# An attention layer over sorted edges: parts of 96, 51 and 40 groups in two stacked tables instead of three parts of 165, 142 and 96

## The chip, the cores and the metric

One Trainium2 chip; the kernel runs on one of its eight cores. The metric is the device time of one execution in microseconds (us). A core has a matmul engine (PE, with a weight load of its own, PEld), a vector engine (DVE), a scalar engine (ACT), GpSimd (POOL) and a queue that only issues transfers (SP); sixteen DMA engines move the bytes between HBM and the on-chip memory.

## The reference

A graph layer with 12,500 nodes of 128 features and 412,500 edges, sorted by target node:

```python
q = x @ Wq + bq;  k = x @ Wk + bk;  v = x @ Wv + bv;  h = x @ Wn + bn
eh = edge_attr @ We + be                                   # 64 -> 128 features
hmid = leaky_relu(concat([q[src], k[dst], eh]) @ A1 + b1, 0.2)
scores = leaky_relu(hmid @ A2 + b2, 0.2)                   # 8 heads
w = softmax(scores.mean(-1), axis=0)                       # over all edges
out = segment_sum(w[:, None] * v[dst], src, num_segments=n)
y = layernorm(h + out) * gamma + beta
return layernorm(x + y)
```

The softmax runs over all edges, and the sum goes back to the *source* node, while the edges come sorted by *target*. So the kernel has to sort 412,500 records by source.

## The kernel before

**Two streams of work.** *Making* goes through the edges in 403 groups of 1024 (`make`, one pass of six steps a group). For a group it loads the edge features (`eat`), a window of 128 rows of the k and v table (`kvs`) and target indices (`dstb`), multiplies them with one-hot matrices on PE (`pkv`), copies the product with ACT into a record buffer (`rec`, six of them, four tiles of 128 records each; L946 and L947), and POOL scatters each tile with an indirect DMA into a table in HBM (`rtab`, L958): eight scatters a group. A record is 260 floats. The table has 98 stretches, one for each block of source nodes, and each stretch has room for a number of tiles of 128 records. Where in its block's stretch a record goes is counted as the edges pass (`count`, `masked`, `places` on PE and DVE).

*Summing* (`sums_of`) reads the tables back. A *unit* is three blocks with the same `t` tiles each (15 tiles for `t` of 5, 12 for `t` of 4; the last unit of a round has two blocks). For a unit SP loads the records (`rt`), the q rows (`qs`), the old partial sum (`old`) and a row of source indices (`rowB`). PE, ACT and DVE then work in pieces of four tiles: the hidden layer (`ph`, `hm`), the scores (`psc`), a running maximum (`mx`, `m`, `ref`), the exponentials (`w`), and the weighted sum by source (`ohs`, `ohw`, `psm`), which is added to `old` and stored to `atab`. In the code, `lags` and `last_lags` give for each kind of instruction the step at which it stands, by the number of four-tile pieces `nk`.

**Parts and rounds.** Records can't all wait until the end, so making is cut into *parts* (`PARTS`, in groups), and a part's stretch of a table is read back in *rounds*. A part's last number is its end; the numbers ahead of it are *stops*, at which the first tiles of every block are surely full and a round may already read them. Part 0 and 2 use table 0, part 1 table 1 (`p % TABS`). What lies beyond a block's own records in a part's last round is masked (`masks`, made in `ended` at the part's end); in the first two parts, which find the tables unwritten, the last tiles of each stretch are filled with zeros beforehand (`fill`, from `empty` on chip or `zeros` in HBM). A part's end also closes one matmul accumulation of counts (`pc`) and opens the next, with the check of limits between (`ended`, `begin`).

**What sets the order.** Everything is in program order on each engine; no scheduler moves it. The summing steps are spread over the making steps: a round begins at its stop or end, or when the round before it is through at 12 tiles a group, whichever is later:

```python
free_at = max(free_at, g)
begun.append(free_at)
free_at += sum(len(bs) * t + 2.4 for q, bs, _ in units if q == p) / PACE
```

With 33 units a round that is 39.3 groups for `t` = 4 and 47.4 for `t` = 5. Rounds begin at groups 74, 140, 187.4, 234.8, 278, 317.3, 367 and 406.3, so 8% of round 6 and the whole of round 7 are left when making ends; these steps run alone, as the *tail*. In the tail a copy of `x + beta` for the end is also made (`rows_x`, `moved`, `put_x`: 14 pieces, 12 steps apart), and then `closing` normalizes and writes the output. During the first groups, before the first round, making runs beside the *preparation*: the q, k, v and h tables (`tables`) and the edge lists (`later`), spread over nine tenths of the groups up to the first stop, and the fills.

The text speaks of these lines of the kernel before: L818, L827, L838 (SP loads of making), L572 (fills), L800 and L880 (counts on PE), L931 and L936 (making on PE), L946 and L947 (record copies on ACT), L958 (scatters), L1144, L1159, L1198, L1356, L1404 (SP's transfers of a unit), L1188 (`slT`), L1224 and L1233 (hidden layer), L1258 (scores), L1284 (heads), L1299 (maximum of a unit), L1305, L1314 and L1323 (reference and weights), L1375 (weighted sum), L1468 (copies of `x`), L1699 (subtractions in the preparation).

Of the kernel before, what the change touches and what calls it, by code (L numbers as in the profile page):

```python
# [21 lines left out]
P = 128  # L22
# [6 lines left out]
GT = 8  # L29
# [3 lines left out]
ROWS = 3  # L33
XA = 3
SPAN = 42
PARTS = (74, 140, 165), (225, 278, 307), (367, 403)
NP = len(PARTS)
NR = sum(map(len, PARTS))
PACE = 12
TABS = 2  # L40
# [9 lines left out]
class Plan:  # L50
# [4 lines left out]
    def __init__(self, n, e, nb, groups):  # L55
        self.n, self.e, self.nb, self.groups = n, e, nb, groups
        at = lambda c: groups * c // 403
        ends = [at(part[-1]) for part in PARTS]
        self.parts = list(zip([0] + ends[:-1], ends))

        def means(g0, g1):
            return [
                (min(e, g1 * GT * P) - g0 * GT * P) * max(0, -(-(n - b) // nb)) / n
                for b in range(nb)
            ]

# [14 lines left out]
        self.lo = [[(most - f) * P for f in fill] for fill in self.fill]  # L81
        self.gate = max(
            g for g in range(self.parts[0][1])
            if all(m + 4.5 * m**0.5 <= lo for m, lo in zip(means(0, g), self.lo[0]))
        )

        self.rounds = []
        for p, (g0, g1) in enumerate(self.parts):
            t0 = 0
            for g in map(at, PARTS[p][:-1]):  # L90
                t = int(min(m - 4.4 * m**0.5 for m in means(g0, g)) // P) - t0
                assert t > 0
                self.rounds.append((p, g, t0, t))
                t0 += t
            self.rounds.append((p, g1, t0, self.tiles[p] - t0))

    def bounds(self):

        first = np.arange(self.nb + 1) * self.cap
        out = [first] * NP  # L100
        for p, g, t0, t in self.rounds:
            full = np.array([(t0 + t) * P] * self.nb + [0])
# [369 lines left out]
def sorted_path(  # L472
# [22 lines left out]
    rtab = [dram.tile([plan.rows, WR], FP, name=f"rtab{k}") for k in range(TABS)]  # L495
# [292 lines left out]
    pcs = {}  # L788
    ready, made_rows = {}, [1]
    masks, placed, lims = {}, {}, {}  # L790
    last_rounds = [r for r, q in enumerate(plan.rounds) if q[1] == plan.parts[q[0]][1]]
    for t in sorted({plan.rounds[r][3] for r in last_rounds}):
        placed[t] = const.tile([P, t], FP, name=f"placed{t}")
# [11 lines left out]
    def make(p):  # L805
# [136 lines left out]
        def evacuate(g, j, pk):  # L942
# [11 lines left out]
            for h in range(2):  # L954
                for i in range(2):
                    t = h * (GT // 2) + j + i
                    nc.gpsimd.nop()
                    one_tile = nc.gpsimd.indirect_dma_start(  # L958
                        out=rtab[p % TABS][:, :],
                        out_offset=bass.IndirectOffsetOnAxis(ap=idxs[g][:, t : t + 1], axis=0),  # L960
                        in_=rec[:, i, h, :], in_offset=None,
                    ).ins
# [143 lines left out]
    def sums_of(bp):  # L1106
# [32 lines left out]
        def load(i):  # L1139
            r, bs, t = units[i]  # L1140
            cap, n, m = plan.cap, plans[i][0], len(bs)
            p, _, t0, _ = plan.rounds[r]
            rt = (late["blk"] if spare_buffer(i) else bp).tile([P, TM, WR], FP, name="rt")
            rows_in = nc.sync.dma_start(  # L1144
                out=rt[:, :n, :].rearrange("p (u t) w -> p u (t w)", u=m),
                in_=rtab[p % TABS][bs[0] * cap : (bs[0] + m) * cap, :]
                .rearrange("(u c) w -> u c w", u=m)[:, t0 * P : (t0 + t) * P, :]
                .rearrange("u (p t) w -> p u (t w)", p=P),
            ).ins
            of_part = [k for k, q in enumerate(plan.rounds) if q[0] == p]  # L1150
            for k in range(of_part.index(r) + 1, len(of_part)):
                tc.declare_no_dep(rows_in, group=f"rows{p}.{k}", reason="tiles that are full")
            tc.add_to_no_dep_group(f"loads{p}.{of_part.index(r)}", rows_in)
            state[i] = dict(rt=rt, hm={}, oh={}, sel={})

        def load_q(i):
# [755 lines left out]
```

## Time and profile before

| | |
|---|---|
| median of 3 runs | 4827.88 us (4826.07 to 4830.85) |
| the profiled execution | 4829.19 us, span 4827.2 us |
| busy share of the span | PE 83%, PEld 64%, DVE 84%, ACT 65%, POOL 68% |
| first and last scatter | 59.3 and 4282.7 us |
| first and last unit's maximum (L1299) | 932.2 and 4685.8 us |
| mean granted clock of PE | 0.916 of full speed |
| DMA | 1484.41 MB, mean 308 GB/s |

The profiled execution is one of its own, with a trace; its span runs from the first to the last instruction. PE's busy share is a sum of modelled matmul ends, so it is an upper figure. Rows of groups read: line, engine, operation, tiles written and read, form, count | busy us, mean ns | idle before, and who ended it. Rows of waits read: who waited for whom: us in total, times, longest. A share over the span mixes three stages: making alone, making beside summing, and the tail.

### The profile page before, as it was taken

What the parts mean: (1) busy time and instruction counts of PE and PEld (TensorE: products, weight loads), DVE (VectorE), ACT (ScalarE), POOL (GpSimd) and SP (SyncE); (2) the same over time, 40 slices, a digit from 0 to 9 for tenths busy, and PEclk for the clock granted to TensorE, in tenths of its full rate; (3) what the DMA queues carried; (4) which work ended last, traced back from release to release, by engine and by line L of the source; (5) the groups of instructions that cost most, each with busy time, mean ns of one, the idle gap of its engine ahead of it and who ended that gap; (6) DMA issues with size and microseconds to landing.
All of it is one profiled execution on the core that took longest, in us unless ns stands there. A gap on an engine that the chain in (4) does not pass through costs nothing. (4 is left out here: it accounts for less than half of the span.)

```text
span 4827.2 us, 84360 instructions
## 1 busy us (share of the span) xinstructions
PE 3991.6 (83%) x26680; PEld 3111.2 (64%) x26680; DVE 4064.7 (84%) x8217; ACT 3144.8 (65%) x8198; POOL 3304.4 (68%) x3279
## 2 busy tenths in 40 slices
PE   3556655577788999999999999998998899998997
PEld 2334433466666777777777666666777777666777
DVE  8878886688878999999998888888999988877767
ACT  2432222366666778787787777777777777777886
POOL 3777777777777777777777777777777777741103
PEclk7877785899888999999999999999999999999999
DMA  6888887888988999999999999999999999989964
GB/s 196 282 279 288 286 298 243 294 300 298 296 299 299 358 336 334 333 348 337 323 335 324 329 331 329 332 336 325 342 332 326 333 316 334 320 294 327 318 215 176
DMA packets 599153, 1484.41 MB, mean 308 GB/s; under 512 B 100352, under 2 KB 299923, under 8 KB 596902
## 3 DMA queue, kind: packets, MB, share of 16 engines
q1 hardware_dynamic: 436350, 1049.04, 65.4%
q0 software_dynamic: 154752, 429.39, 23.3%
q8 instruction: 212, 3.47, 0.3%
q14 instruction: 247, 2.02, 0.1%
q10 hardware_dynamic: 7592, 0.48, 0.1%
HBM read 906.61 MB, written 611.06 MB: 314 GB/s over the span
## 5 line engine op out<-in xcount | busy, mean ns | idle before, releaser
L958 POOL DMA_INDIRECT rtab<-rec,idx x3224 | 3219.2, 999 | 1061.2 <-issue 777.2
L946 ACT ACTIVATE rec<-pkv 128x1024 f32<-128x1024 f32 x806 | 822.2, 1020 | 1120.4 <-DMA rtab<-rec,idx 572.8
L1346 ACT ACTIVATE ohw<-ohs,w 128x128 f32<-128x128 bf16 x3626 | 1189.1, 399 | 75.7 <-DVE ohs L1332 27.2
L1375 PE MATMUL psm<-rt,ohw 128*128 128x128 f32 x7252 | 1023.1, 285 | 1.1 <-ACT ohw L1346 1.0
L1375 PEld LDWEIGHTS psm<-rt,ohw 128*128 128x128 f32 x7252 | 943.9, 197 | 76.1 <-ACT hm L1243 7.7
L936 PE MATMUL pkv<-WeS,eat 128*128 128x256 f32 x3224 | 946.4, 421 | 0.0
L1247 DVE TENSOR_TENSOR hm<-ph,hm 128x512 f32<-128x512 f32 (+1 forms) x949 | 627.4, 661 | 300.9 <-ACT hm L1243 299.0
L931 PE MATMUL pkv<-kvs,ohd 128*128 128x256 bf16 x3224 | 539.1, 295 | 373.6 <-ACT rec L946 370.2
L931 PEld LDWEIGHTS <-ohd 128*128 128x128 bf16 x3224 | 320.9, 105 | 645.9 <-issue 531.8
L936 PEld LDWEIGHTS pkv<-WeS,eat 128*128 128x128 f32 x3224 | 620.2, 214 | 75.0
L1224 PE MATMUL ph<-ident,rt 128*128 128x128 f32 x3626 | 587.2, 284 | 64.5 <-DVE hm L1247 63.6
L1210 DVE TENSOR_SCALAR ohT<-rowB,iotaP,power 128x512 bf16<-128x512 uint8 (+2 forms) x1274 | 598.9, 492 | 34.8 <-DMA rowB<-row 34.6
L1243 ACT ACTIVATE hm<-ph 128x512 f32<-128x512 f32 (+1 forms) x949 | 537.5, 566 | 84.1 <-PE ph L1233 29.2
L1224 PEld LDWEIGHTS ph<-ident,rt 128*128 128x128 f32 x3626 | 418.3, 146 | 269.7 <-issue 145.5
L1233 PE MATMUL ph<-ohT,qs 128*128 128x512 bf16 (+2 forms) x2548 | 559.7, 323 | 16.1 <-DVE ohT L1210 11.3
L872 DVE TENSOR_SCALAR ohd<-dstb,node 128x1152 bf16<-128x1152 uint8 x404 | 565.0, 1399 | 4.5 <-PE pkv L931 4.5
L900 DVE TENSOR_TENSOR ats<-pc,oh 128x792 f32<-128x792 f32 x403 | 392.2, 973 | 61.7 <-PE pc L880 56.6
L1332 DVE TENSOR_TENSOR ohs<-iotaE,sl 128x512 bf16<-128x512 bf16 (+1 forms) x949 | 404.6, 426 | 5.0 <-ACT ohw L1346 4.8
L862 DVE TENSOR_REDUCE few<-oh 128x99 bf16<-128x792 bf16 x403 | 395.1, 980 | 13.9
L911 DVE TENSOR_REDUCE pos<-ats 128x8 f32<-128x792 f32 x403 | 390.7, 970 | 2.5
L1258 PE MATMUL psc<-hm,A2s 128*32 128x512 f32 (+1 forms) x1898 | 345.9, 607 | 31.9 <-DVE hm L1247 23.7
L1284 PEld LDWEIGHTS psm<-headsum,z 96*128 96x128 f32 (+2 forms) x2112 | 259.7, 193 | 32.8 <-issue 8.3
(190 smaller groups left out, 3790.5 us busy)
## 6 DMA issues: line engine op xcount, KB each, us to landing
rt<-rtab SPq DMA_DIRECT2D x160, 1950.0 KB
rt<-rtab SPq DMA_DIRECT2D x96, 1560.0 KB
eat<-in_ea SPq DMA_DIRECT2D x201, 512.0 KB
rtab<-rec,idx POOLq DMA_INDIRECT x3224
dstb<-dtab SPq DMA_DIRECT2D x201, 256.0 KB
qs<-qtab SPq DMA_DIRECT2D x256, 192.0 KB
atab<-old SPq DMA_DIRECT2D x256, 192.0 KB
old<-atab SPq DMA_DIRECT2D x224, 192.0 KB
```

Source lines behind the costliest of these rows:

```text
L872: nc.vector.tensor_scalar(to, row[:, cols], node, None, op0=ALU.is_equal)
L931: nc.tensor.matmul(pk[:, i, h, :], ohd[t], kvs, start=(h == 0), stop=False,)
L936: nc.tensor.matmul(pk[:, i, :, :D], eat[:, (j + i) * P : (j + i + 1) * P], WeS, start=False, stop=True,)
L946: nc.scalar.activation(rec[:, :, :, : 2 * D], pk, AF.Copy)
L958: one_tile = nc.gpsimd.indirect_dma_start(out=rtab[p % TABS][:, :], out_offset=bass.IndirectOffsetOnAxis(ap=idxs[g][:, t : t + 1], axis=0) ...
L1210: nc.vector.tensor_scalar(st["oh"][k][:, (a - t0) * P : (b - t0) * P], st["rowB"][:, a * P : b * P], iotaP, power[:, bs[u] : bs[u] + 1], o ...
L1224: nc.tensor.matmul(ph[:, j * P : (j + 1) * P], st["rt"][:, t0 + j, :D], ident, is_transpose=True, start=(j == 0), stop=False,)
L1233: nc.tensor.matmul(ph[:, cols], st["qs"][:, j0 // t, s, :], oh[:, cols], start=False, stop=(s == 1 and j1 == t0 + n),)
L1243: nc.scalar.activation(hm, state[i]["ph", k][:, : n * P], AF.Copy, scale=SLOPE)
L1247: nc.vector.tensor_tensor(hm, ph[:, : n * P], hm, op=ALU.max)
L1346: nc.scalar.activation(ohw[:, j, :], ohs[:, :, j], AF.Copy, scale=st["w"][:, t0 + j : t0 + j + 1])
L1375: nc.tensor.matmul(st["psS"][:, (1 + u) * P : (2 + u) * P], ohw[:, j, :], st["rt"][:, t0 + j, D : 2 * D], start=(k == 0), stop=(k == t - 1),)
```

## The change

Seven parts take the place of three. They end at groups 96, 192, 243, 283, 323, 363 and 403; the first two have a stop each, at 60 and 156. Rounds go from eight to nine, with 4, 5, 4, 5, 5, 4, 4, 4 and 4 tiles a block (before 5, 5, 5, 4, 4, 5, 4, 5): 39 tiles a block instead of 37, 297 units instead of 264. Stretches of a table are 9 tiles long instead of 15. Part 3 lies in table 0 above part 2's five tiles, part 5 in table 1 above part 4's four (`TABLE`, `ABOVE`); part 6 goes to the bottom of table 0. Since parts that share a table use different tiles, their scatters and loads are declared free of each other (`apart`). There are seven masks in two buffers instead of three in one. The first load of a part's last round waits for the last eight scatters of the part. The gate, the group from which scatters of part 0 must see its fills, moves from 120 to 54. The fills are 98 pieces of three tiles for two blocks each; before, 22 of the first 49 had four tiles. The unit with two blocks and four tiles takes the lags of a twelve-tile unit.

By the rule above, rounds begin at groups 60, 99.3, 156, 195.3, 243, 290.4, 329.7, 368.9 and 408.2; 87% of round 7 is through when making ends.

```diff
-PARTS = (74, 140, 165), (225, 278, 307), (367, 403)
+PARTS = (60, 96), (156, 192), (243,), (283,), (323,), (363,), (403,)
 NP = len(PARTS)
+TABLE = (0, 1, 0, 0, 1, 1, 0)
+ABOVE = (0, 0, 0, 5, 0, 4, 0)
...
-        most = max(self.tiles)
+        most = max(t + above for t, above in zip(self.tiles, ABOVE))
...
+        while any(abs(self.gate - g) < 6 for _, g, *_ in self.rounds):
+            self.gate -= 1
...
+    def apart(self, p, q):
+        a, b = ABOVE[p], ABOVE[q]
+        return p != q and TABLE[p] == TABLE[q] and (
+            a >= b + self.tiles[q] or b >= a + self.tiles[p]
+        )
...
-    maskp = pool("mask", 1)
+    maskp = pool("mask", 2)
...
-                        out=rtab[p % TABS][:, :],
+                        out=rtab[TABLE[p]][:, :],
...
+                    for q in range(NP):
+                        for k in range(len(PARTS[q]) if plan.apart(p, q) else 0):
+                            for name in "rows", "loads":
+                                tc.declare_no_dep(
+                                    one_tile, group=f"{name}{q}.{k}", reason="other tiles"
+                                )
...
+                    tail_of[p].append(one_tile)
...
-            o = lags(p, nk)
+            o = lags(p, max(nk, 3))
...
+            t0 += ABOVE[p]
...
+            if r == of_part[-1]:
+                for one in tail_of[p][-GT:]:
+                    tc.add_manual_dep(rows_in, one.name, ...)
```

Three places show what moves. First, SP's queue during the preparation, some 33 to 50 groups in. Before, with `rtab_76` and `rtab_77` the two tables, `htab`, `qtab` and `xt` the node tables' transfers:

```order
L572 DMA rtab_76<-empty 128x2x1040
L1748 DMA htab<-ns_4025 128x7x128
L1749 DMA qtab<-sq 128x1792
L1711 DMA xt<-in_xT 128x896
L572 DMA rtab_77<-zeros 128x2x780
L822 TENSOR_LOAD start
L827 ISA
L827 DMA kvs<-kvtab 128x256
L838 DMA dstb<-dtab 128x2048
L572 DMA rtab_76<-empty 128x2x1040
L818 DMA eat<-in_ea 128x1024
```

Now, with the tables named `rtab_77` and `rtab_78`:

```order
L1783 DMA htab<-ns_3006 128x7x128
L1784 DMA qtab<-sq 128x1792
L1746 DMA xt<-in_xT 128x896
L588 DMA rtab_77<-empty 128x2x780
L588 DMA rtab_78<-zeros 128x2x780
L835 DMA eat<-in_ea 128x1024
L839 TENSOR_LOAD start
L844 ISA
L844 DMA kvs<-kvtab 128x256
L588 DMA rtab_77<-empty 128x2x780
```

Fills and tables stand closer together: a group's loads have about one and a half fills beside them instead of one. Second, SP's queue where a part's last round begins. Before, round 5 (part 1, at group 318 of making), each row with the semaphores that it waits for (`DMASW` are POOL's scatters, `DMAHW` other transfers):

```order
L1198 DMA rowB<-row 128x1536 [waits DMAHW7_49,DMAHW4_49,DVE_49]
L1144 DMA rt<-rtab_77 128x3x1300 [waits DMAHW0_49,DMASW7_49,PE_49]
L1404 DMA atab_72<-old 128x384 [waits DMAHW1_49,DVE_49]
L1356 DMA old<-atab_71 128x384 [waits DMAHW2_49]
L822 TENSOR_LOAD start
```

Now, round 4 (part 2, at group 243 of making, the part's own end):

```order
L1233 DMA rowB<-row 128x1920 [waits DMAHW3_49,DMAHW2_49,DVE_49]
L1169 DMA rt<-rtab_77 128x3x1300 [waits DMASW4_49,DMASW5_49,DMASW3_49,DMASW6_49,DMASW2_49,DMASW7_49,DMASW1_49,DMAHW4_49,DMASW0_49,PE_49]
L835 DMA eat<-in_ea 128x1024 [waits DMAHW5_49]
L839 TENSOR_LOAD start
L844 ISA
L844 DMA kvs<-kvtab 128x256 [waits DMAHW7_49]
```

The load waits for all eight scatter semaphores instead of one, and `eat` and `kvs` stand behind it. Third, PE in the last round, about one unit's rows. Before, fifteen tiles:

```order
L1305 MATMUL psm<-ident,mx 128x128
L1375 MATMUL psm<-rt,ohw 128x128 x4
L1258 MATMUL psc<-hm,A2s 32x512 x3
L1258 MATMUL psc<-hm,A2s 32x384
L1224 MATMUL ph<-ident,rt 128x128 x4
L1233 LDWEIGHTS qs
L1233 MATMUL ph<-ohT,qs 128x128
L1233 LDWEIGHTS qs
L1233 MATMUL ph<-ohT,qs 128x128
L1233 LDWEIGHTS qs
L1233 MATMUL ph<-ohT,qs 128x384
```

Now, twelve tiles:

```order
L1410 MATMUL psm<-rt,ohw 128x128 x4
L1293 MATMUL psc<-hm,A2s 32x512 x3
L1340 MATMUL psm<-ident,mx 128x128
L1259 MATMUL ph<-ident,rt 128x128 x4
L1268 LDWEIGHTS qs
L1268 MATMUL ph<-ohT,qs 128x512
L1268 LDWEIGHTS qs
L1268 MATMUL ph<-ohT,qs 128x512
L1410 MATMUL psm<-rt,ohw 128x128 x4
```

A piece of four tiles is now one block, so its q rows take two matmuls of 512 columns instead of up to four shorter ones; the maximum's matmul moves behind the scores.

More of the change, by code (lines that the diff above doesn't have):

```diff
@@ L70, in __init__ @@
         ]
-        most = max(self.tiles)
+        most = max(t + above for t, above in zip(self.tiles, ABOVE))
+        assert TABLE[:TABS] == (0, 1) and not any(ABOVE[:TABS])
+        assert all(t + a <= self.tiles[k] for t, a, k in zip(self.tiles, ABOVE, TABLE))
         self.cap = most * P
@@ L95, in __init__ @@
             self.rounds.append((p, g1, t0, self.tiles[p] - t0))
+        while any(abs(self.gate - g) < 6 for _, g, *_ in self.rounds):
+            self.gate -= 1
     def bounds(self):
-        first = np.arange(self.nb + 1) * self.cap
-        out = [first] * NP
+        at = np.arange(self.nb + 1)
+        starts = [at * self.cap + P * t * (at < self.nb) for t in ABOVE]
+        out = starts[:]
         for p, g, t0, t in self.rounds:
+            first = starts[p]
             full = np.array([(t0 + t) * P] * self.nb + [0])
@@ L790, in sorted_path @@
     masks, placed, lims = {}, {}, {}
+    tail_of = [[] for _ in plan.parts]
     last_rounds = [r for r, q in enumerate(plan.rounds) if q[1] == plan.parts[q[0]][1]]
@@ L1145, in load @@
                 out=rt[:, :n, :].rearrange("p (u t) w -> p u (t w)", u=m),
-                in_=rtab[p % TABS][bs[0] * cap : (bs[0] + m) * cap, :]
+                in_=rtab[TABLE[p]][bs[0] * cap : (bs[0] + m) * cap, :]
                 .rearrange("(u c) w -> u c w", u=m)[:, t0 * P : (t0 + t) * P, :]
@@ L1152, in load @@
                 tc.declare_no_dep(rows_in, group=f"rows{p}.{k}", reason="tiles that are full")
+            for q in range(NP):
+                for k in range(len(PARTS[q]) if plan.apart(p, q) else 0):
+                    tc.declare_no_dep(rows_in, group=f"rows{q}.{k}", reason="other tiles")
             tc.add_to_no_dep_group(f"loads{p}.{of_part.index(r)}", rows_in)
+            if r == of_part[-1]:
+                for one in tail_of[p][-GT:]:
+                    tc.add_manual_dep(
+                        rows_in, one.name, mybir.DependencyInfo(
+                            mybir.DependencyClass.Sync, mybir.DependencyReason.DATA
+                        ), reason="records of the part",
+                    )
             state[i] = dict(rt=rt, hm={}, oh={}, sel={})
```

## The prediction

> **What bounds the kernel now.** I read the page first, then the scatter line by stretches, then the waits of single rounds, then the tail by stretches. From the page: engine totals, bytes by fortieths, and the costliest group.
>
> ```profile
> PE 3991.6 (83%) x26680; PEld 3111.2 (64%) x26680; DVE 4064.7 (84%) x8217; ACT 3144.8 (65%) x8198; POOL 3304.4 (68%) x3279
> ...
> GB/s 196 282 279 288 286 298 243 294 300 298 296 299 299 358 336 334 333 348 337 323 335 324 329 331 329 332 336 325 342 332 326 333 316 334 320 294 327 318 215 176
> ...
> L958 POOL DMA_INDIRECT rtab<-rec,idx x3224 | 3219.2, 999 | 1061.2 <-issue 777.2
> ```
>
> No engine is full over the span, but POOL's 3224 scatters, eight to a group of 1024 edges, set the pace while edges are read. The scatter line by stretches (columns: stretch, length, busy and count, clock, DMA share, GB/s):
>
> ```profile
> 60.00:360.00 300.00, 232.36 (x209) 0.78 0.85 278
> 360.00:720.00 360.00, 276.29 (x272) 0.74 0.88 291
> ...
> 2030.00:2520.00 490.00, 374.88 (x378) 0.97 0.95 335
> 2520.00:2980.00 460.00, 351.07 (x358) 0.97 0.94 326
> 2980.00:3180.00 200.00, 152.50 (x156) 0.98 0.95 333
> 3180.00:3380.00 200.00, 148.78 (x150) 0.99 0.94 330
> 3380.00:3900.00 520.00, 397.08 (x401) 0.98 0.95 330
> 3900.00:4040.00 140.00, 107.06 (x109) 0.98 0.95 333
> 4040.00:4284.00 244.00, 178.16 (x181) 0.98 0.91 319
> ```
>
> Counting eight scatters to a group, the stretches from 2030 on are rounds 2, 3, 4 (two halves), 5 and 6 (two pieces). Length over count is 1.296, 1.285, 1.282, 1.333, 1.297, 1.284 and 1.348 us. So a scatter comes every 1.285 us, 10.3 us a group, whatever else runs, except in the preparation (first two rows) and in the second part of rounds 4 and 6. Those two are the rounds with the most units: twelve-tile units at 33/39.3 = 0.84 a group; round 3 has 33/43.2 = 0.76. The waits of three windows tell why (who waited, for whom: us in total, times, longest): of 100 to 450, of 2980 to 3380, and of 3900 to 4284.
>
> ```profile
> ACT rec L946 <- DMA rtab<-rec,idx: 148.3, 33, 9.9
> ```
>
> ```profile
> POOL rtab L958 <- ACT rec L947: 5.4, 8, 2.0
> ...
> POOL rtab L958 <- ACT slT L1188: 4.3, 5, 3.1
> ...
> PE pc L800 <- DVE high L990: 3.5, 1, 3.5
> ```
>
> ```profile
> ACT rec L946 <- DMA rtab<-rec,idx: 8.8, 10, 3.1
> ...
> POOL rtab L958 <- ACT rec L947: 8.5, 13, 2.5
> ...
> POOL rtab L958 <- ACT slT L1188: 6.4, 6, 4.8
> ```
>
> Six `rec` buffers stand between ACT and POOL, 24 scatters or 31 us of work. Early, ACT waits for a buffer to come free: the queue is full and POOL alone is late. In rounds 4 and 6 POOL waits for ACT's copies: the queue has run dry, and the engines that make records and work off units in turn are late. That is the threshold on which this case turns: about 0.84 twelve-tile units a group is too much, 0.76 is not, and the full queue covers the first 14 to 20 groups (109/8 and 156/8).
>
> After the last scatter only units run. Stages of all engines (PE, weight loads, DVE, ACT, POOL, then clock, DMA share, GB/s), and the units counted at the line that reduces each unit's maximum:
>
> ```profile
> 60.00:720.00 660.00, 385.32 (x1480) 266.78 (x1480) 535.24 (x847) 222.15 (x309) 508.65 (x480) 0.76 0.87 285
> ...
> 3900.00:4284.00 384.00, 355.94 (x2434) 271.71 (x2433) 331.01 (x669) 280.72 (x784) 285.21 (x289) 0.98 0.93 324
> 4290.00:4560.00 270.00, 243.15 (x1794) 186.18 (x1793) 193.62 (x475) 209.17 (x617) 30.27 (x14) 0.96 0.91 317
> 4560.00:4680.00 120.00, 116.69 (x953) 95.12 (x951) 89.83 (x245) 111.24 (x327) 0.00 (x0) 1.00 0.69 235
> ```
>
> ```profile
> 4284.00:4364.00 80.00, 1.33 (x8) 0.92 0.87 290
> 4364.00:4560.00 196.00, 3.04 (x18) 0.98 0.92 327
> 4560.00:4690.00 130.00, 2.36 (x14) 0.99 0.65 218
> ```
>
> That is 40 units in about 402 us: 8 left over (10.0 us each), 18 beside the copies of `x` for the end (10.9), 14 alone (9.3, PE 97% busy).
>
> **The change, part by part.**
>
> *Unit cost.* Tiles a block go from 37 to 39, units from 264 to 297: twelve-tile ones from 99 to 198, fifteen-tile ones from 165 to 99. What does PE pay for each? The matmuls of a unit while twelve-tile units ran (2970 to 3200), then in the tail of fifteen-tile ones (4540 to 4680):
>
> ```profile
> L1375 PE MATMUL psm<-rt,ohw 128*128 128x128 f32 x429 | 60.1, 284 | 0.2 <-ACT ohw L1346 0.2
> ...
> L1224 PE MATMUL ph<-ident,rt 128*128 128x128 f32 x216 | 33.8, 279 | 3.5 <-DVE hm L1247 3.5
> L1233 PE MATMUL ph<-ohT,qs 128*128 128x512 bf16 x106 | 31.5, 379 | 1.8 <-DVE ohT L1210 1.8
> ...
> L1258 PE MATMUL psc<-hm,A2s 128*32 128x512 f32 x106 | 24.4, 630 | 5.1 <-DVE hm L1247 3.0 <-ACT slT L1188 2.2
> ```
>
> ```profile
> L1375 PE MATMUL psm<-rt,ohw 128*128 128x128 f32 x445 | 59.6, 275 | 0.0
> L1224 PE MATMUL ph<-ident,rt 128*128 128x128 f32 x212 | 34.4, 282 | 0.0
> L1233 PE MATMUL ph<-ohT,qs 128*128 128x256 bf16 (+2 forms) x170 | 32.3, 299 | 0.7 <-DVE ohT L1210 0.7
> L1258 PE MATMUL psc<-hm,A2s 128*32 128x512 f32 (+1 forms) x112 | 15.7, 578 | 0.5 <-DVE hm L1247 0.5
> ```
>
> Busy over count, times the matmuls of one unit: twelve tiles have 24, 12, 6 and 6, so 3.36 + 1.88 + 1.78 + 1.38 = 8.4; fifteen have 30, 15, 12 and 8, so 4.02 + 2.43 + 2.28 + 1.12 = 9.9. The ratio is 0.85, and with the heads and maxima, which both units have alike (estimate 1.4 each), 0.87. By tiles it would be 0.80: a twelve-tile unit is dear.
>
> *Tail.* Making ends with round 7 at (403 - 368.9)/39.3 = 87% (before: round 6 at 92%), so about 42 units follow the last scatter, not 40, all of twelve tiles. Left over: 8.7 at 9.5 us (10.0 before held a change from twelve to fifteen tiles) = 83. The last round's 33: 9.3 x 0.87 = 8.1 alone, 10.9 x 0.87 = 9.5 beside the copies, which fill 14 x 12/6 = 28 units instead of 21 and so weigh three quarters as much: I take 9.2, so 304. Sum 387 against 402: **-15**. Ends: 8.1 throughout with 8.7 x 10.0 left over gives 354, -48; 9.7, near the 10.0 of the leftover row, gives 407, +5.
>
> *Rounds 5, 6, 7* (groups 290 to 403) are twelve-tile rounds at 0.84 in a row, 113 groups; before, only rounds 4 and 6 were, 75 groups, each behind a lighter one that refilled the queue. Dry, a scatter takes (1.333 + 1.348)/2 - 1.285 = 0.056 us longer, 0.44 a group. After 13 covered groups 100 x 0.44 = 44 us; before's own loss was 150 x 0.048 + 181 x 0.063 = 18.6. Net **+25**; ends -19 (none runs dry) and +31 (no group covered).
>
> *Rounds 3 and 4* (95 groups of fifteen-tile units at 0.69) follow the twelve-tile round 2 (39 groups), which uses up the queue that the light round 1 (0.58) fills. Round 2 of before ran such units at 1.296, so 0 to 0.011 x 8 x 95 = 8 us; I take **+5**.
>
> *Preparation.* Tables and edge lists now go into 54 groups instead of 66, the fills of `rtab` into 52 and 78 groups instead of 72 and 147. In the first 720 us the excess over 1.285 is 209 x 0.150 + 272 x 0.039 = 42 us. Why? One scatter of POOL and the DVE instruction beside it:
>
> ```profile
> 242.74 2.20 POOL L958 DMA_INDIRECT rtab<-rec,idx  x1 [0.30 <-issue]
> ```
>
> ```profile
> 242.10 2.02 DVE L1699 TENSOR_TENSOR less<-ns,sp 128x1792 f32<-128x1792 f32 x1
> ```
>
> The scatter took 2.20 us against a mean of 0.999 while DVE subtracted two SBUF tiles. The number of these subtractions stays, so that part of the 42 stays too. But bytes crowd: the fills, by the DMA list,
>
> ```profile
> rtab<-zeros SPq DMA_DIRECT2D x49, 780.0 KB
> ...
> rtab<-empty SPq DMA_DIRECT2D x22, 1040.0 KB
> ```
>
> went at 45.0/72 + 39.1/147 = 0.89 MB a group and now go at 39.1/52 + 39.1/78 = 1.25; tables (estimate 43.6 MB from their shapes) 0.65, now 0.81. On 285 GB/s x 10.9 us = 3.1 MB that makes 3.6 MB a group, 331 GB/s, below the 358 of the fullest slice. Ends 0 and +42 (the excess doubles); I take **+10**.
>
> The Trainium skill (SBUF — State Buffer, Who interferes with whom) says that a `tensor_tensor` on VectorE takes only the read side of the port pair that it shares with GpSimd, and infers that descriptor writing goes on beside it. By that the 42 us would come from the transfers and grow with them, 42 x 3.6/3.1 = 49, an estimate of +7 in place of 0 at the low end. The trace disagrees: 2.20 us stands beside the subtraction.
>
> *Round 0* starts at group 60 at 0.84 instead of 0.50, with fill 1 running to group 86: an estimate of 3.85 MB a group, against 358 GB/s x 10.3 = 3.7, so 0 to (3.85/0.358/1000 - 0.0103) x 1000 x 26 = 11; **+5**. Its first load waits for the stop's records, in both kernels; SP in 860 to 900:
>
> ```profile
> SPq L1144 <- DMA rtab<-rec,idx: 28.4, 1, 28.4
> ```
>
> Queued behind it are the next `eat`, `kvs` and `rowB`. Four groups lie loaded ahead (41 us), so it is covered, at no cost, while that holds; if not, the price is at most those 28 us.
>
> *Part changes* rise from two to six. Each holds PE up to 3.5 us (the `pc` row above): 0 with a full queue, all of it dry. 4 x 3.5 = 14 at most; **+5**. Masks, limits and the larger `mask` pool are a few instructions each: nothing, beside POOL; without that cover some 6 us in all.
>
> Sum: -15 + 25 + 5 + 10 + 5 + 5 = **+35**. The profiled execution took 4829.19 us (span 4827.2), 1.3 over the median of 4827.88. So 4864 in its terms, **4863** as a median.
>
> **The rivals.**
> - *PE has room, and the dry rounds were something else* (faster). Then rounds 5 to 7 hold 1.285 as round 5 of before nearly did: -19 for that term, 0 for rounds 3 and 4: 35 - 44 - 5 = -14, **4814**. It decides if a scatter still comes every 1.29 us after group 330. For it: weight loads fill only 271.71 of 384 us in round 6. Against it: POOL's waits for ACT there. The Trainium skill (Perfetto Trace Analysis, Identifying the Most-Contended Engine) says matmul busy time is no measure of a full TensorE and weight-load time is one; by that 71% leaves room, and this rival holds. The trace bears it out only in part, since matmuls and loads wait in one order with DVE and ACT.
> - *The tail gains in full* (no change): 8.1 a unit, -48 instead of -15: +2, **4830**. For it: 97% busy PE with short waits at the end. Against: the shorter lags of a three-chunk last round leave less time between maximum and weights.
> - *Transfers bind* (much slower): preparation +42, round 0 +11, part changes +14, rounds 5 to 7 +31, the others as above: +88, **4916**. For it: shares of 0.94 to 0.95 now. Against: 358 GB/s was reached once.
>
> **How the numbers follow.** A change within 0.2% (9.7 us) can't be told from none here. Forecast (4838 to 4895) 0.50; PE has room 0.20; tail in full 0.16; transfers 0.14. The range 4798 to 4920 takes in all four as they stand and leaves out the combined ends (4829 - 48 - 19 below, every upper end above), under 2 in 10. Faster 0.21, same 0.17, slower 0.62: the first rival with a hundredth for the edges of the forecast, the second likewise, the rest. The forecast's own range is 4838 to 4895.
>
> **What would show it.** Scatters at 1.33 to 1.35 us from about group 305 to 403, with POOL waiting for ACT's record copies and ACT hardly for `rec`; a tail of 42 units in 375 to 400 us; 60 to 720 us with some 470 scatters. Wrong would be: a queue that stays filled to the end, or a tail of 350 us.

## The result and the profile after

The changed kernel takes 4890.92 us (median of 4, 4884.45 to 4893.84) against 4826.98 us for the kernel before: a ratio of 1.013, 95% interval 1.0112 to 1.0148. It is slower by 64 us, inside the range and 28 us above the 4863 forecast. The profiled execution took 4892.69 us with a span of 4890.9, so 63.7 us more span than before. From its page, the scatter group:

```profile
L975 POOL DMA_INDIRECT rtab<-rec,idx x3224 | 3225.5, 1000 | 1155.0 <-issue 755.4
```

The 3224 scatters (L958 before, L975 now) are as short as they were: 3225.5 us of work against 3219.2. It is the idle time ahead of them that grew, from 1061.2 to 1155.0 us. POOL is fed later, not slower. The scatter line by stretches, cut where groups 60, 100, 160, 200 and 290 begin (columns: stretch, length, busy and count, clock, DMA share, GB/s), first before:

```profile
59.20:720.80 661.60, 509.93 (x480) 0.76 0.87 285
720.80:1133.60 412.80, 315.28 (x320) 0.78 0.82 280
1133.60:1753.60 620.00, 473.74 (x480) 0.91 0.92 313
1753.60:2166.10 412.50, 314.98 (x320) 0.98 0.96 339
2166.10:3096.20 930.10, 710.40 (x720) 0.97 0.95 330
3096.20:4283.70 1187.50, 894.91 (x904) 0.98 0.94 328
```

and after:

```profile
59.80:733.30 673.50, 515.33 (x480) 0.77 0.92 299
733.30:1173.00 439.70, 314.14 (x320) 0.92 0.95 331
1173.00:1792.90 619.90, 473.56 (x480) 0.97 0.90 312
1792.90:2217.00 424.10, 315.86 (x320) 0.96 0.94 326
2217.00:3151.30 934.30, 712.48 (x720) 0.98 0.97 336
3151.30:4383.80 1232.50, 894.11 (x904) 0.97 0.93 321
```

Row by row the lengths differ by +11.9 (preparation), +26.9 (round 0), -0.1 (round 1 from group 100), +11.6 (round 2), +4.2 (rounds 3 and 4) and +45.0 us (rounds 5 to 7). With that the last scatter moves from 4282.7 to 4382.8 us. The tail gives part of it back. The line that reduces a unit's maximum (L1334, before L1299), for the leftover units and the last round, in the changed kernel:

```profile
4384.00:4471.00 87.00, 1.32 (x8) 0.94 0.80 273
4471.00:4755.00 284.00, 5.47 (x33) 0.99 0.81 288
```

With one more at 4383.0, 42 units follow the last scatter, and the last maximum comes 367.7 us after it; before it was 403.1 us for 40: -35.4. The lone last round goes at 8.7 us a unit (33 of them from 4471.8 to 4750.5).

The waits where the queue of records runs dry, from 3200 to 4280 (who waited, for whom: us in total, times, longest), of the engines and then of SP's queue:

```profile
ACT rec L963 <- DMA rtab<-rec,idx: 53.2, 35, 4.5
POOL rtab L975 <- ACT rec L964: 26.9, 27, 5.2
```

```profile
SPq L1233 <- DMA row<-slT: 593.4, 84, 9.7
```

POOL waits for ACT's copies, as foreseen. SP stands 593 of 1080 us, 7 us for each of 84 units, at the load of `rowB`, until ACT's row of indices has landed in HBM. Every load written behind it waits too. The stand alone doesn't set the two kernels apart: in the same window of the kernel before it is 533.4 us, in 78 waits. What it costs has to be found by moving it (e6).

A useful measure of the queue, worked out from start and end times in the traces, is how long after the end of ACT's second copy into a buffer (L964, before L947) the last of the buffer's four scatters begins. With the queue full it is about 24 us, with an empty one 4.1. Before, it fell to 10.7 us when round 0 began, and was back at 23 after five groups. Now it falls to 4.1 at group 61 and stays between 4 and 9 until group 100; from group 290 to 403 its mean is 4.9.

### The profile page after: what moved, and what is told of

Same layout as the page of the kernel before. It is cut to its first block, busy times and chain, and to the rows that moved or that the text cites. A ratio compares the mean times of both kernels' runs of the same rounds, so it can differ in the third digit from the quotient of the medians.

```text
span 4890.9 us, 86496 instructions
## 1 busy us (share of the span) xinstructions
PE 4105.9 (84%) x27209; PEld 3177.6 (65%) x27507; DVE 4139.7 (85%) x8395; ACT 3217.6 (66%) x8558; POOL 3310.2 (68%) x3280
## 5 line engine op out<-in xcount | busy, mean ns | idle before, releaser
L975 POOL DMA_INDIRECT rtab<-rec,idx x3224 | 3225.5, 1000 | 1155.0 <-issue 755.4
L1381 ACT ACTIVATE ohw<-ohs,w 128x128 f32<-128x128 bf16 x3822 | 1251.1, 399 | 98.6 <-DVE ohs L1367 57.7
L1410 PE MATMUL psm<-rt,ohw 128*128 128x128 f32 x7644 | 1075.5, 284 | 3.8 <-ACT ohw L1381 3.4
L1410 PEld LDWEIGHTS psm<-rt,ohw 128*128 128x128 f32 x7644 | 989.1, 196 | 89.6 <-ACT ohw L1381 9.5
L1282 DVE TENSOR_TENSOR hm<-ph,hm 128x512 f32<-128x512 f32 x981 | 658.0, 671 | 295.0 <-ACT hm L1278 293.2
L953 PE MATMUL pkv<-WeS,eat 128*128 128x256 f32 x3224 | 905.1, 407 | 0.0
L1245 DVE TENSOR_SCALAR ohT<-rowB,iotaP,power 128x512 bf16<-128x512 uint8 (+3 forms) x1176 | 593.7, 519 | 41.0 <-DMA rowB<-row 40.5
L1278 ACT ACTIVATE hm<-ph 128x512 f32<-128x512 f32 x981 | 560.3, 571 | 59.0 <-PE ph L1268 20.9
L1293 PE MATMUL psc<-hm,A2s 128*32 128x512 f32 (+1 forms) x1962 | 392.1, 602 | 37.5 <-DVE hm L1282 33.0
L1367 DVE TENSOR_TENSOR ohs<-iotaE,sl 128x512 bf16<-128x512 bf16 x981 | 416.1, 424 | 1.0 <-ACT ohw L1381 1.0
L917 DVE TENSOR_TENSOR ats<-pc,oh 128x792 f32<-128x792 f32 x403 | 392.3, 974 | 22.9 <-PE pc L897 21.3
L1358 ACT ACTIVATE w<-S,ref 128x12 f32<-128x12 f32 (+3 forms) x297 | 89.7, 302 | 375.6 <-DVE ref L1349 368.0
```

Of the source, the lines that this page charges most:

```text
L953: nc.tensor.matmul(pk[:, i, :, :D], eat[:, (j + i) * P : (j + i + 1) * P], WeS, start=False, stop=True,)
L975: one_tile = nc.gpsimd.indirect_dma_start(out=rtab[TABLE[p]][:, :], out_offset=bass.IndirectOffsetOnAxis(ap=idxs[g][:, t : t + 1], axis=0) ...
L1245: nc.vector.tensor_scalar(st["oh"][k][:, (a - t0) * P : (b - t0) * P], st["rowB"][:, a * P : b * P], iotaP, power[:, bs[u] : bs[u] + 1], o ...
L1278: nc.scalar.activation(hm, state[i]["ph", k][:, : n * P], AF.Copy, scale=SLOPE)
L1282: nc.vector.tensor_tensor(hm, ph[:, : n * P], hm, op=ALU.max)
L1381: nc.scalar.activation(ohw[:, j, :], ohs[:, :, j], AF.Copy, scale=st["w"][:, t0 + j : t0 + j + 1])
```

## Experiments

The ratio is that to the kernel before on the same chip. The last three columns are worked out from start times in each run's trace. These and the stretches below are one execution each, on chips whose medians of the kernel before differ by up to 12 us.

| run | ratio (95%) | median us | last scatter us | units after it | tail us |
|---|---|---|---|---|---|
| before | 1 | 4823 to 4836 by chip | 4282.7 | 40 | 403.1 |
| after | 1.0130 (1.0112 to 1.0148) | 4890.92 | 4382.8 | 42 | 367.7 |
| e1 half of q | 1.0139 (1.0110 to 1.0168) | 4898.08 | 4389.3 | 42 | 364.3 |
| e2 few edge loads | 1.0042 (1.0025 to 1.0059) | 4847.32 | 4335.8 | 42 | 365.9 |
| e3 loose steps | 1.0481 (1.0461 to 1.0500) | 5064.21 | 4544.3 | 42 | 379.3 |
| e4 late rounds | 1.0153 (1.0120 to 1.0185) | 4909.55 | 4382.2 | 44 | 391.9 |
| e5 thin edge loads | 1.0052 (1.0035 to 1.0069) | 4851.01 | 4346.5 | 42 | 368.2 |
| e6 later spread | 1.0043 (1.0027 to 1.0059) | 4845.06 | 4338.9 | 42 | 364.9 |
| e7 spread from ACT | 1.0212 (1.0184 to 1.0240) | 4918.19 | 4399.5 | 42 | 367.9 |
| e8 pace 11 | 1.0240 (1.0223 to 1.0257) | 4938.44 | 4282.0 | 57 | 516.2 |
| e9 = e5 and e6 | 1.0026 (1.0010 to 1.0043) | 4848.24 | 4332.9 | 42 | 368.4 |
| e10 = e6, pace 13 | 1.0161 (1.0142 to 1.0179) | 4907.51 | 4426.0 | 37 | 329.1 |
| e11 before, later spread | 0.9979 (0.9968 to 0.9990) | 4822.45 | 4281.2 | 40 | 398.3 |
| e12 before, later spread, pace 13 | 1.0077 (1.0060 to 1.0094) | 4867.62 | 4339.8 | 37 | 380.6 |

The theories. A, the prediction's: the engines that make records and work off units in turn, PE first, have too much to do. B: loads come late, because of their bytes (B1) or because SP stands ahead of them (B2). C: too few steps lie between what a unit needs and its use.

**e1, less work on PE.** One of the two matmuls with q in each piece of the hidden layer is left out, so the hidden layer isn't the reference's.

```diff
-                for s in range(2):
+                for s in range(1):
...
-                        stop=(s == 1 and j1 == t0 + n),
+                        stop=(j1 == t0 + n),
```

> The changed kernel without the second half of q in the hidden layer: one of two q matmuls of every piece is left out, so the low bits of q are missing from the output. Everything else stays, transfers and ACT and DVE work too. Theory A (the rounds of twelve-tile units run dry because a unit holds PE and the engines in turn with it for too long): a unit loses three matmuls of 512 columns, 0.9 us, at 0.84 units a group 0.75 us, more than the 0.4 to 0.6 us a group by which the dry rounds are late. Scatters in rounds 5 to 7 come back to about 1.29 us, making gets 60 to 80 us shorter, the tail 42 x 0.5 to 0.9 = 20 to 35, total about 4790 to 4815. Theory B (transfers bind): making and tail stay within 10 us, about 4880. Theory C (ACT and DVE wait for one another because twelve-tile units leave too few steps between maximum, reference and weights): less than 20 us gained, since those waits stay.

All engines from 3200 to 3600 (PE, weight loads, DVE, ACT, POOL, clock, DMA share, GB/s), first of the changed kernel, then of e1, and e1's scatters from group 290 to the end:

```profile
3200.00:3600.00 400.00, 367.58 (x2471) 280.09 (x2503) 346.42 (x687) 286.36 (x796) 290.58 (x293) 0.98 0.93 322
```

```profile
3200.00:3600.00 400.00, 354.74 (x2378) 272.50 (x2379) 344.54 (x686) 283.21 (x789) 285.49 (x291) 0.96 0.93 321
...
3157.30:4390.30 1233.00, 893.82 (x904) 0.96 0.94 321
```

PE has 12.8 us less to do in 400, though the granted clock is lower, and the stretch of 113 groups takes 1233.0 us instead of 1232.5. PE's work is not the bound: theory A in that form falls.

**e2, an eighth of the loads of edge features**, so most groups use old ones.

```diff
-            if g % 2 == 0:
+            if g % 16 == 0:
```

> The changed kernel with one load of edge features in eight: the other groups multiply the same loaded features, so the records are wrong, but every matmul and copy stays. 0.23 MB of some 3.5 MB a group are gone. Theory A: the dry rounds stay dry; 0 to 15 us gained, most of it in the preparation. Theory B (transfers bind in rounds 0, 2 and 5 to 7): 6.5% fewer bytes bring a scatter from 1.36 back to 1.29 us, 50 to 80 us gained, about 4820 to 4840. Theory C: as theory A.

```profile
729.40:1160.60 431.20, 314.25 (x320) 0.93 0.93 315
...
3134.00:4336.80 1202.80, 892.29 (x904) 0.98 0.91 308
```

Rounds 5 to 7 lose 30 of their 45 us and round 0 loses 8.5 of 27. That speaks for theory B, though this edit takes away bytes and places in SP's queue together.

**e3, more steps for a twelve-tile unit** between what was suspected to follow too closely.

```diff
-        L, e = 2 * nk, 1
+        L, e = 2 * nk, 1 + int(nk < 4)
```

> The changed kernel with one step more between the stages of a twelve-tile unit (the lag e of three-piece rounds 2 instead of 1), but not in the last round. Work and transfers stay. Theory A: within 15 us of the changed kernel. Theory C: ACT's waits for DVE's reference (368 us over the span) fall to half or less while edges are made, rounds 5 to 7 come near 1.30 us a scatter, and the time falls by 30 to 60 us. Theory B: no change.

Its waits from 3200 to 4300 and its last stretch of scatters:

```profile
POOL rtab L975 <- ACT rec L964: 111.0, 59, 5.2
...
PE psc L1293 <- ACT slT L1223: 96.8, 69, 3.6
```

```profile
SPq L1169 <- PE psm L1410: 117.4, 56, 5.4
```

```profile
3217.20:4545.30 1328.10, 893.44 (x904) 0.94 0.90 298
```

Looser steps keep buffers longer: the single `psc` bank is waited for by PE, the records' buffers by SP, and all twelve-tile rounds get worse (groups 60 to 100 take 475.8 us, 160 to 200 451.3). The wait that the edit was to remove, ACT's for the reference, hardly fell, first in the changed kernel (from 3200 to 4280), then in e3:

```profile
ACT w L1358 <- DVE ref L1349: 127.7, 66, 3.8
```

```profile
ACT w L1358 <- DVE ref L1349: 112.8, 62, 5.4
```

So theory C has nothing for it here, but it isn't ruled out either: this edit didn't do what would test it.

**e4, rounds 0 and 4 begin three groups later**, so that SP's stand at round 0's first load should go.

```diff
-        free_at = max(free_at, g)
+        free_at = max(free_at, g + (3 if p in (0, 4) else 0))
```

> The changed kernel with rounds 0 and 4, which begin at the very group at which their stop or part ends, begun three groups later (63 and 246), so that SP doesn't wait for scatters still queued in POOL. If the dry round 0 (groups 60 to 100 took 27 us more than before) comes from SP's stand at the first load, groups 60 to 100 get 15 to 25 us shorter. If it comes from the number of units and the fills beside them, the gain is under 8 us. Elsewhere nothing changes but a shift of three groups, which adds at most a few us in the rounds behind.

Round 0 and the last rounds by the scatter line:

```profile
735.20:1157.30 422.10, 315.31 (x320) 0.92 0.95 327
...
3140.40:4383.20 1242.80, 895.40 (x904) 0.97 0.92 317
```

The stretch of groups 60 to 100 gets 17.6 us back, though three of its groups have fewer units beside them now. SP's list no longer has the stand, but by the measure above the queue still runs dry in this round, at group 76 (4.3 us) instead of 61. Every later round is pushed back, two more units are left over (24 us), and the end can't be told from that of the changed kernel: the intervals overlap.

The next four are aimed at bytes, SP's order and pace.

**e5, fewer bytes.** All loads of edge features stay where they are, and each but the first three moves 64 of 512 columns.

```diff
-                eat = eap.tile([P, 2, EG // 2], FP)
-                nc.sync.dma_start(out=eat[:, :m, :], in_=ea[:, g : g + m, :])
+                k = g // 2
+                if k < 3:
+                    eats.append(eap.tile([P, 2, EG // 2], FP, name="eat"))
+                eat = eats[k % 3]
+                c = EG // 2 if k < 3 else EG // 16
+                nc.sync.dma_start(out=eat[:, :m, :c], in_=ea[:, g : g + m, :c])
```

> The changed kernel with all 201 loads of edge features issued where they were, with the same waits, but each after the third moves only 64 of 512 columns (0.03 MB a group instead of 0.26); the products of the edge features are therefore not those of the reference. Theory B1 (bytes: the sixteen DMA engines at 0.93 to 0.96 are what the dry rounds wait for): as with the eighth of the loads, 4840 to 4860 us, groups 290 to 403 at 10.6 to 10.7 us. Theory B2 (SP's order: loads stand behind SP's waits, whatever their size): no change from the changed kernel, 4880 to 4900 us, groups 290 to 403 at 10.8 to 11.0.

```profile
3138.80:4347.50 1208.70, 893.99 (x904) 0.98 0.91 306
```

24 of the 45 us are gone with every issue in its place. But the waits changed with the bytes. From 3200 to 4280 SP's stand at these loads, most of it ended by PE, falls from 73.6 to 10.8 us in all, and its stand for the row of indices (L1237 there, L1233 in the changed kernel) goes from 593.4 to 631.2:

```profile
SPq L1237 <- DMA row<-slT: 631.2, 84, 12.1
```

So e5 doesn't show that the bytes by themselves cost anything, nor that they cost by making the row late.

**e6, SP's order alone.** Transfers and bytes are the same; `rowB` of a twelve-tile unit is spread two steps later.

```diff
-            turned=-turn + 1 + e, spread=-turn + 3 + 2 * e, q=-9, onehot=-1 - e, sloped=1,
+            turned=-turn + 1 + e, spread=-turn + 3 + 2 * e + 2 * (nk < 4), q=-9,
+            onehot=-1 - e, sloped=1,
```

> The changed kernel with the spread of a unit's row of indices (rowB) put two steps later in the units of twelve tiles, before the last round: only SP's order changes, the transfers are the same. B2 (SP stands about 7 us in each unit for the row in HBM, and the loads behind it come late): 15 to 45 us faster, 4845 to 4876. B1 (bytes): no change, 4880 to 4900. A third: the one-hot rows on DVE now wait for rowB, which has three steps instead of five, and the units fall behind: slower, 4900 to 4950.

Scatters of round 0 and of the last rounds, and SP's waits from 3200 to 4280:

```profile
732.20:1160.00 427.80, 314.37 (x320) 0.95 0.97 342
...
3130.60:4339.90 1209.30, 897.03 (x904) 0.98 0.94 327
```

```profile
SPq L1439 <- DVE m L1348: 358.0, 76, 8.1
...
SPq L1233 <- DMA row<-slT: 70.0, 60, 3.3
```

SP's stand for the row falls from 593.4 to 70.0 us. SP now stands at a unit's store instead (358.0 us), later in its order. The last rounds take 1209.3 us: 23 of the 45 are gone, at a higher rate of bytes (327 GB/s instead of 321). Who waited for the records of a unit, in the changed kernel and in e6, from 3200 to 4280:

```profile
  DVE sl L1208: 32.2, 25
```

```profile
  DVE sl L1208: 14.3, 18
```

That fits a link: with SP standing, `rt` is asked for late, DVE waits for it, and whatever stands behind that on DVE, the making of records too, waits along. It is read from the waits and not shown by itself. SP isn't freed by the edit: all its stands in this window come to 752 us in the changed kernel and 745 in e6. What changes is which transfers stand behind them.

**e7, the spread issued by ACT.**

```diff
-            nc.sync.dma_start(
+            nc.scalar.dma_start(
                 out=st["rowB"][:, : nt * P],
```

> The changed kernel with the spread of every unit's row of indices issued by ACT instead of SP: SP no longer stands for that row, ACT does, three to four steps after it has written the row itself. B2: SP's loads come early, groups 290 to 403 near 10.4, 20 to 50 us faster, 4840 to 4870. B1: no change from SP's side. In either, if the row isn't through when ACT comes to it, ACT stands some 1 to 3 us a unit, and the copies of records behind it are late: up to 297 x 2 = 600 us slower.

From 3163 to 4401:

```profile
POOL rtab L975 <- ACT rec L964: 50.8, 44, 3.5
...
DVE ohT L1245 <- DMA rowB<-row: 41.5, 28, 3.5
...
DVE sl L1208 <- DMA rt<-rtab: 9.0, 8, 2.8
```

SP is free of the row, and DVE's wait for records is down to 9.0 us (32.8 in the changed kernel, from 3151 to 4384). Yet groups 290 to 403 take 1237.0 us: this wait alone doesn't decide. DVE now waits 41.5 us for `rowB`, which ACT asks for, and POOL waits 50.8 us for ACT instead of 31.1. That these two eat the gain is argued from the list, not shown.

**e8, a slower pace**: 0.77 twelve-tile units a group instead of 0.84.

```diff
-PACE = 12
+PACE = 11
```

> The changed kernel with the rule of begins at 11 tiles a group instead of 12 (twelve-tile units at 0.77 a group): every round takes 9% more groups, round 7 begins near group 388 and about 54 units follow the last scatter instead of 42. If the pace of units is what the queue runs dry on (the prediction's threshold between 0.76 and 0.84), groups 290 to 403 go at 10.3 to 10.4, which gives 45 to 60 us back (with rounds 0 and 2 some 70 to 80), and the tail takes 12 x 8.7 = 104 longer: 4910 to 4950 us. If the loss has nothing to do with the pace, making stays as it is and the time is 4980 to 5000.

```profile
731.70:1145.40 413.70, 315.16 (x320) 0.94 0.98 344
...
1764.30:2178.80 414.50, 317.02 (x320) 0.98 0.93 326
...
3113.00:4283.00 1170.00, 894.69 (x904) 0.97 0.93 322
```

Nearly every loss after the preparation is gone (groups 200 to 290 keep their 4 us). Groups 60 to 100 take 413.7 us (before 412.8, after 439.7), and the last scatter is at 4282.0, as in the kernel before. So the pace decides, at the place that the prediction gave it: 0.77 is sustained, 0.84 not. The tail pays 148.5 us for fifteen more units, 9.9 each, and making gives back 100.8, 6.7 each. SP's waits from 731 to 1146 in this run:

```profile
SPq L1233 <- DMA row<-slT: 181.4, 30, 9.9
...
SPq L1169 <- DMA rtab<-rec,idx: 28.3, 1, 28.3
```

The stand at the first load is still there, 28.3 us, and empties the queue down to 4.1 us just as it does in the changed kernel. At this pace the queue is back at 14 us by group 95. Nor is the stand for the row shorter in the last rounds, from 3200 to 4280, where the queue holds 21 us in the mean:

```profile
SPq L1233 <- DMA row<-slT: 581.6, 79, 11.3
```

Neither stand costs anything by itself; each costs where the pace leaves no room to recover. And 344 GB/s at a DMA share of 0.98 went with scatters every 1.293 us, while the changed kernel's 331 at 0.95 went with 1.374: the transfers don't bind by their rate there.

**e9, e5 and e6 together.**

> The changed kernel with both edits together: rowB two steps later in twelve-tile units, and loads of edge features of 64 columns instead of 512 after the third (so the edge products are not the reference's). Alone they took 46 and 40 us off. If bytes cost only because they make the row of indices late, on which SP stands with the next loads behind it, they are one cost: 4835 to 4850 us. If bytes and SP's stand are two costs, they add: 4795 to 4815, groups 290 to 403 at 10.35 to 10.5 us.

```profile
3134.80:4333.90 1199.10, 898.60 (x904) 0.99 0.92 308
```

By the ratios the edits alone are worth 38 us (1.0130 - 1.0052, of 4827) and 42, together 50. They don't add in full: in the last rounds e5 took off 24 us, e6 23 and both 33. What the two share is not shown; that fewer bytes shorten the stand for the row is not it, by e5's list. 29 us against e8's 1170.0 remain in the last rounds with both. Only the pace removed those, and what they wait for is left open.

**e10, e6 with 13 tiles a group**, 0.91 units.

```diff
-PACE = 12
+PACE = 13
...
+            turned=-turn + 1 + e, spread=-turn + 3 + 2 * e + 2 * (nk < 4), q=-9,
```

> The changed kernel with rowB two steps later in twelve-tile units and the rule of begins at 13 tiles a group instead of 12 (twelve-tile units at 0.91 a group). Some 34 units instead of 42 follow the last scatter. At 11 tiles a group 15 units went from making to the tail and cost 148 us there, 9.9 each, and gave back 101, 6.7 each. If that holds on the other side, 8 units moved into making give 8 x 3.2 = 25 us: about 4820, as fast as the kernel before. If the queue runs dry more steeply at 0.91, making pays 9 or more a unit: 4845 to 4880.

```profile
733.40:1188.10 454.70, 317.27 (x320) 0.94 0.96 331
...
3200.50:4427.00 1226.50, 896.29 (x904) 0.98 0.95 326
```

Against e6 the tail saves 35.8 us for five units and making pays 87: units moved forward cost 17 each there. 37 units follow the last scatter, where 34 were expected. So the price of a unit beside making rises with the pace: 6.7 us between 11 and 12 tiles a group, 17 between 12 and 13 (with e6's edit), against 7 to 10 in the tail.

**e11, the kernel before with e6's edit.**

> The kernel before, with rowB two steps later in twelve-tile units alone. Its two dry stretches (groups 290 to 330 and 369 to 403, at 10.59 and 10.64 instead of 10.32 us) cost some 22 us together. If SP's stand makes them, as it made 23 of 60 us in the last three rounds of the changed kernel, 5 to 15 us faster than before: 4809 to 4819. If the stand matters only behind the changed kernel's rounds, no change, 4818 to 4828.

```profile
3106.20:4282.20 1176.00, 892.70 (x904) 0.98 0.95 329
```

The last 113 groups take 1176.0 us instead of 1187.5. The ratio is 0.9979, 0.9968 to 0.9990: the one version here that is faster than the kernel before, by some 10 us.

**e12, the kernel before, all spreads two steps later, 13 tiles a group.**

```diff
-PACE = 12
+PACE = 13
...
-            turned=-turn + 1 + e, spread=-turn + 3 + 2 * e, q=-9, onehot=-1 - e, sloped=1,
+            turned=-turn + 1 + e, spread=-turn + 5 + 2 * e, q=-9, onehot=-1 - e, sloped=1,
```

> The kernel before with rowB two steps later in all units ahead of the last round, and 13 tiles a group instead of 12: some 35 units follow the last scatter instead of 40. By 3.2 us for a unit moved, and the stand of SP gone: 5 x 3.2 + 5 to 15, so 4795 to 4805 us, faster than both kernels. If fifteen-tile units at 0.75 a group run the queue dry too, or their one-hot rows wait for rowB, 4825 to 4860.

```profile
1752.10:2187.30 435.20, 317.10 (x320) 0.99 0.96 335
...
3136.50:4340.80 1204.30, 898.45 (x904) 0.98 0.95 327
```

Groups 160 to 200, fifteen-tile units here, go from 412.5 to 435.2 us. So they run dry too, at 0.75 units a group by the rule of begins. They hardly wait for `rowB`, which the edit also moved (from 1752 to 2187):

```profile
DVE ohT L1210 <- DMA rowB<-row: 3.1, 4, 0.9
```

So the pace is the likelier cause, though no run here has it alone. The rule's 12 was near the edge for both kernels.

## Why the prediction was right or wrong

| term | predicted | measured |
|---|---|---|
| tail | -15 (-48 to +5) | -35.4 |
| rounds 5 to 7 | +25 (-19 to +31) | +45.0 |
| rounds 3 and 4 | +5 (0 to 8) | +4.2 |
| preparation | +10 (0 to 42) | +11.9 |
| round 0 | +5 (0 to 11) | +26.9 |
| round 2 | 0 | +11.6 |
| part changes | +5 (0 to 14) | within the rows above |

The sign, the two largest terms and the threshold (0.84 units a group is too much, 0.76 is not) were right; e8 shows the threshold, with 0.77. That the sum came within 28 us is in part luck: rounds 5 to 7, round 0 and round 2 missed by 20, 22 and 12 us on one side, the tail by 20 on the other. So four terms were wrong.

*Round 0* missed by most: "Four groups lie loaded ahead (41 us), so it is covered, at no cost, while that holds". The stand was counted on SP alone. The waits from 733 to 1173 show who stood with it, and below them the same wait before, from 720 to 1134:

```profile
DVE sl L1206 <- DMA rt<-rtab: 60.8, 13, 33.1
...
PE psc L1216 <- DVE sl L1206: 28.9, 2, 26.6
```

```profile
DVE sl L1171 <- DMA rt<-rtab: 35.2, 3, 28.9
```

DVE comes to the first unit's indices and waits 33.1 us for records that SP hasn't asked for, and PE waits 26.6 behind DVE. The groups that lay loaded were on the chip, but the making that uses them stands behind these waits in the order of DVE and PE. So the queue of records empties in one go. Before, it filled again beside a round at 0.50 units; now 0.84 follows, and the price is 27 us: not the stand's length, but the dry groups up to 100. The stand is only part of it. In e4, without the stand, these groups still took 9.3 us more than before (422.1 against 412.8). The prediction had a price for that, 0.44 us a group after 13 covered ones, some 11 us for a round of 39 groups at 0.84, but used it for rounds 5 to 7 alone. That the loss lies just below the 28 us named for the uncovered case is luck: those counted SP's stand, not dry groups.

*Rounds 5 to 7* had the right mechanism, a queue that runs dry at this pace, and the wrong size and cause. No group was covered by a full queue, where 13 were counted: in groups 286 to 290 the measure stood at 5.5 us. And a dry group took 10.91 us in the mean (1232.5 / 113), not 10.72. By start times groups 300 to 320 went at 10.68 and 370 to 390 at 10.64, near the prediction's price, but 290 to 300 at 11.50 and 320 to 326, around the end of a part, at 11.7; what makes these dearer is not shown. PE's work doesn't make the loss (e1). SP's order makes about half of it (23 of the 45 us, e6), and the rest is open. The rival with room on PE was right about PE: the Trainium skill (Perfetto Trace Analysis, Identifying the Most-Contended Engine) takes weight-load time as the measure, and 280.09 of 400 us with e1's outcome agree that TensorE wasn't full. But its conclusion, that scatters then hold 1.285 us, did not follow. Of the other two rivals, the tail gave 35.4 of the 48 us, and no run shows that transfers bind: e8 had 344 GB/s without a loss, and e5 leaves it open.

*Round 2* had no term. In the kernel before such units ran in round 3 at 0.76; at 0.84 the queue that round 1 filled lasts only to about group 185. By the 0.44 us it is some 11 us again, and 11.6 were measured.

*The preparation* came out near its +10, but the reason isn't borne out. Its scatters took 5.4 of the 11.9 us longer by themselves (515.33 against 509.93 of POOL's time), and e5, with 0.23 MB a group less there too, took 672.9 us against 673.5.

*The tail* was mis-sized the other way: the last round took 8.7 us a unit, not 9.2. By start times it is 8.9 beside the copies of `x` and 7.8 for the last seven units, where 9.5 and 8.1 stood; the nine units left over took 89 us where 83 stood. *Part changes* hold PE somewhat longer than the 3.5 us taken, here from 3400 to 4300:

```profile
PE pc L817 <- DVE high L1014: 6.5, 2, 4.5
```

Of the signs named, POOL waiting for ACT's record copies came true, and the tail fell just short of its 375 to 400 us. From group 290 a scatter came every 1.363 us, above 1.33 to 1.35. That ACT would hardly wait for `rec` is not what the list says (53.2 us). But by the start times ACT's copies between groups 300 and 398 begin at least 22.9 us after the last scatter from the same buffer has ended, while with a full queue (groups 100 to 160) 3.4 us are enough. So the buffer was most likely free, and what ended these waits is not shown.

## What to carry to other kernels

When two streams share in-order engines, price a stand of the transfer queue by what waits for the transfer on every engine, and by whether the stream that falls behind has spare pace afterwards: a stand of 28 us cost nothing where it could be made up (e8); where it couldn't, it emptied the queue fifteen groups before the pace would have done so (e4). Before cutting work finer, look in the transfer queue's own list of waits for the dearest stand and for what stands behind it; moving one load two steps back in that order was worth 42 us here, although the queue's stands added up to as much as before. A rule for the pace is worth measuring on both sides: here one tile a group more or less cost some 50 us.

## What the runs showed of the hardware

- Fewer bytes went with a gain in e5, where SP's waits changed too; a higher load (0.98 share, 344 GB/s in e8) did no harm. The share of busy DMA engines said nothing on which rounds were late: 0.93 in the last rounds of the changed kernel, 0.93 in e8, which lost nothing there.
- A row of 1.5 KB from ACT to HBM, read back by a load that SP issues, held SP's queue 7 us a unit in the mean and 9.7 at most (593.4 us in 84 waits).
- With 3.5% of PE's busy time taken out (354.74 instead of 367.58 of 400 us), the granted clock (0.96 instead of 0.98) and the time stayed nearly where they were.
- Long scatters go with DVE's subtractions of two SBUF tiles (L1699, up to 2.03 us): of the 46 scatters over 1.5 us in the kernel before, against a mean of 0.999, 32 overlap most with such a subtraction.
